# Interleaving the block sums of A21 and A22, and a different pair of first matmuls, in a Strassen-like interaction kernel

## The chip, the cores and the metric

The kernel runs on one core of a Trainium2 chip. The metric is the device time of one execution in microseconds. The engines are named as the profile names them: PE (TensorE matmul) and PEld (its weight loads), DVE (VectorE), ACT (ScalarE), POOL (GpSimd) and SP (SyncE, which here only issues DMAs).

## The reference

```python
# x: (1024, 512); weight: (64, 512, 512); lin_w: (512, 512); lin_b: (512,); all float32
out_lin = x @ lin_w.T + lin_b
xv = jnp.einsum('bf,efm->bem', x, weight)
zp = jnp.einsum('bf,efm->bem', jnp.square(x), jnp.square(weight))
interaction = 0.5 * jnp.sum(jnp.square(xv) - zp, axis=1)
return out_lin + interaction
```

Per embedding e the kernel needs the product x @ weight[e], squared and summed over the 64 embeddings. The second term is one product, x squared by the sum over e of the squared weights.

## The kernel before

All matrices are float32. The products are done with two nested levels of a Strassen (Winograd) scheme: seven block products instead of eight at each level. The x matrix is cut into four outer blocks; A21 is the one at row 1, column 0 and A22 the one at row 1, column 1. Each outer block has four inner quarters. The kernel numbers the seven left-hand operands of either level "1" to "7": "1", "2" and "4" are blocks as they are, and "5", "6", "7" and "3" are sums:

- "5" = third-row block plus fourth-row block (of a block's quarters: the raw quarter 3 plus quarter "4")
- "6" = "5" minus "1"
- "7" = "1" minus the raw quarter 3
- "3" = "2" minus "6"

So "6" needs "5", and "3" needs "6"; "7" needs only data from memory. The results lie in one resident tile `xs`, by outer and inner number. `inner_x(i)` makes the four inner sums of outer block i (lines L157 to L160, in the order 5, 6, 7, 3). Outer block "4" is A22, so `inner_x("4")` makes the sums of A22. `outer_x(i)` makes the sums of whole blocks (L144 for "5", L146 for "6", L148 for "7", L150 for "3"). All run on DVE except those of block "3", which run on POOL. A21 is not one of the seven outer operands, but the linear part needs its inner sums as well: `a21_sums` makes them on DVE (L227 to L230, tile A_sums).

The weights are handled in 32 pairs q of two embeddings. The right-hand operands come from POOL: `outer_t` makes an outer sum (tile `to`, L324) and `inner_t` the inner sums of one block (tile `ti`, three instructions, L335, L342, L343). The same three lines, called with the transposed linear weight `lw_sb`, make its inner sums `lt_sb`. `ti` and `to` have three buffers each.

The order is written out by hand. `st.at(t, fn)` files a function under a due time, and at the end all functions run in order of due time; each engine then executes its instructions in that order, one after another, waiting on semaphores where a tile needs it. Negative times are the start-up. There the order is:

1. `spin` (-40): matmuls on constants, before any data has arrived (L180 on bf16 ones, L182 on fp32 zeros). Their results are not read.
2. `lin` (-30 and -22): the linear part of the first row of outer blocks, in four PSUM banks lin0 to lin3 (L198); `lin_out` copies them out on ACT (L208).
3. `lin_p` (-14 to -2): the linear part of the second row of outer blocks, by seven products; each has one half from A21 and one from A22 (L244, banks x_lin, v_lin, y_lin). The order is 1, 5, 6, 2, 7, 3, 4. For "5" PE first takes the A21 sum, then the A22 sum. Copies between banks and out of them run on ACT (L258, L278); `lin_join` runs on DVE (L264).
4. from 0 on: the pairs, `product` (L364), with ACT copies (L429, L403, L405) and DVE additions (L408, L424) out of the banks.

The sums have these due times: inner sums of block 1 at -29, of block 2 at -22, of A21 at -20, of A22 at -18, outer and inner sums of block 5 at -16, 6 at -5, 7 at -3. POOL's order at the start is: `lt_sb` sums of both halves (-30, -29), then ti of block 1 of pair 0 (-7.5), to5, ti of block 2, to6, ti of block 6, ti of block 5.

PSUM tiles have tags: x with two buffers, v and y with three each. A tile of a tag waits until the previous holder of its buffer has been read. SP issues the loads of x in the order of `load_x` calls (L113, L109 for A21), A22 last, its raw quarter as the very last; then weights (L303, L306). ACT issues lw_sb (L120) and half of the first weights.

Of the kernel before, what the change touches and what calls it, by code (L numbers as in the profile page):

```python
# [28 lines left out]
def kernel(  # L29
# [30 lines left out]
    nc = tc.nc  # L60
    _, _, _, Q = x.shape
    E, F, M = weight.shape
    P = 128
    NK = F // P
    HM = M // 2
    BK = 2 * HM
# [20 lines left out]
    def xsl(i, o):  # L87
        return xs[:, SLOT[i], SLOT[o], :]
# [10 lines left out]
    a21 = {i: raw_sb[:, n, :] for n, i in enumerate("124")}  # L99
    a21 |= {i: a21_sb[:, n, :] for n, i in enumerate("5673")}  # L100
    A21 = raw_sb[:, 3:7, :]
# [20 lines left out]
    def quarter(r, kk, n):  # L122

        w = slice(0, 3) if n is None else n
        for i, rk in BLOCK.items():
            if rk == (r, kk):
                return a21[i] if n == 3 else xs[:, SLOT[i], w, :]
        return A21[:, w, :]

    def outer_x(i, eng=nc.vector):  # L130
        if i in BLOCK:
            return []

        def put(n):
            w = slice(0, 3) if n is None else n

            def of(o):
                return a21[o] if n == 3 else xs[:, SLOT[o], w, :]

            def src(r, kk):  # L140
                return quarter(r, kk, n)

            if i == "5":
                eng.tensor_add(of(i), src(1, 0), src(1, 1))  # L144
            elif i == "6":
                eng.tensor_sub(of(i), of("5"), src(0, 0))  # L146
            elif i == "7":
                eng.tensor_sub(of(i), src(0, 0), src(1, 0))  # L148
            else:
                eng.tensor_sub(of(i), src(0, 1), of("6"))  # L150

        return [lambda: put(None), lambda: put(3)]

    def inner_x(i, eng=nc.vector):
        add, sub = eng.tensor_add, eng.tensor_sub
        return [
            lambda: add(xsl(i, "5"), a21[i], xsl(i, "4")),  # L157
            lambda: sub(xsl(i, "6"), xsl(i, "5"), xsl(i, "1")),  # L158
            lambda: sub(xsl(i, "7"), xsl(i, "1"), a21[i]),  # L159
            lambda: sub(xsl(i, "3"), xsl(i, "2"), xsl(i, "6")),  # L160
        ]
# [10 lines left out]
    def spin():  # L172

        one = nc.const_aps.tensor(1.0, [P, BK], mybir.dt.bfloat16)
        zero = nc.const_aps.tensor(0.0, [P, BK], F32)
        for n in range(3):
            ps = psum.tile([P, BK], F32, tag="y", name=f"y_spin{n}", bufs=3)
            nc.tensor.matmul(ps, one[:, 0:P], one, start=True, stop=True)  # L180
        for n in (HM, BK):
            nc.tensor.matmul(  # L182
                ps[:, 0:n], zero[:, 0:P], zero[:, 0:n], start=True, stop=True
            )

    def lin(kk):

        order = [(s, j, l) for s in range(2) for j in range(2) for l in range(2)]
        if kk == 0:
            order.sort(key=lambda o: o[2])  # L190
        for s, j, l in order:
            n = 2 * s + j
            if kk == 0 and l == 0:
                tag = "xxvv"[n]
                LIN[n] = psum.tile(
                    [P, M], F32, tag=tag, name=f"lin{n}", bufs=2 if tag == "x" else 3
                )
            nc.tensor.matmul(  # L198
                LIN[n],
                quarter(0, kk, (0, 1, 3, 2)[2 * s + l])[:, ts(j, P)],  # L200
                lw_sb[:, 2 * kk + l, :],
                start=(kk == 0 and l == 0),
                stop=(kk == 1 and l == 1),
            )
# [10 lines left out]
    def lin_x(kk, o):  # L215
        if kk == 1:
            return xsl("4", o)
        return A21[:, SLOT[o]] if o in "124" else A21_SUMS[:, "5673".index(o)]

    def a21_sums():  # L220
        add, sub = nc.vector.tensor_add, nc.vector.tensor_sub

        def of(o):
            return lin_x(0, o)

        return [
            lambda: add(of("5"), A21[:, 3], of("4")),  # L227
            lambda: sub(of("6"), of("5"), of("1")),
            lambda: sub(of("7"), of("1"), A21[:, 3]),
            lambda: sub(of("3"), of("2"), of("6")),  # L230
        ]

    def lin_p(o, bank, first):
# [28 lines left out]
    def lin_join(bank, s, blk):  # L262
# [5 lines left out]
        return fn  # L268

    st.at(-40, spin)  # L270
    for kk in range(2):
        st.at(-30 + 8 * kk, lambda kk=kk: lin(kk))
        st.at(-30 + kk, lambda kk=kk: sums_t(LT[kk], lw_sb[:, ts(kk, 2)]))
# [256 lines left out]
    for sums, t in (  # L530
        (inner_x("1"), -29),
        (inner_x("2"), -22),
        (a21_sums(), -20),
        (inner_x("4"), -18),
        *((outer_x(m) + inner_x(m), t) for m, t in zip("567", (-16, -5, -3))),
    ):
        for n, fn in enumerate(sums):
            st.at(t + 0.1 * n, fn)
# [197 lines left out]
```

## Time and profile before

| what | value |
|---|---|
| median of 3 runs | 1421.06 us (1420.85 to 1421.62) |
| the profiled execution, its own time | 1421.11 us |
| its span, first to last instruction | 1419.3 us |
| PE busy, share of the span | 1410.8 us, 99% |
| DVE, ACT, POOL busy | 923.2, 616.9, 1179.0 us |
| mean DMA rate | 194 GB/s |

An fp32 matmul instruction of the program appears in the trace as two passes, so a product of two halves appears as a group of four. A group's line gives its start, its length, and in brackets the engine's idle time before it with what ended that; matmul ends are modelled and overlap the next start, so the distance between starts is the better measure.[...]

### The profile page before, as it was taken

How to read it: one execution, taken by the hardware profiler on the slowest of the kernel's cores; microseconds unless marked ns; L12 is line 12 of the kernel's file. 1: busy time of each engine (PE TensorE's matmuls, PEld its weight loads, DVE VectorE, ACT ScalarE, POOL GpSimd, SP SyncE). 2: the span in 40 equal slices, each digit the busy share in tenths (PEclk: the TensorE clock that was granted, in tenths of full speed). 3: DMA queues.
4: the chain of work that ended last, by engine and by line, in shares of the span. 5: the costliest groups of instructions: out<-in, count | busy, mean ns of one | idle time of the engine just before them, and what ended most of it. 6: DMA issues, size and time to landing. Idle time of an engine off the chain costs nothing.

```text
span 1419.3 us, 18121 instructions
## 1 busy us (share of the span) xinstructions
PE 1410.8 (99%) x6479; PEld 1232.5 (87%) x6479; DVE 923.2 (65%) x1338; ACT 616.9 (43%) x822; POOL 1179.0 (83%) x1046
## 2 busy tenths in 40 slices
PE   8999999999999999999999999999999999999998
PEld 5888888888888888888888888888888888888887
DVE  6766666666666665666665666665666765666665
ACT  1354443444444444444445444445444345444353
POOL 5688888888888888888888988888888888888884
PEclk9999999999999999999999999999999999999999
DMA  4399888889988889888889888899988899998884
GB/s 178 90 207 207 201 199 200 187 193 215 200 201 200 186 190 217 200 200 201 185 195 214 199 201 200 187 198 210 202 200 199 197 190 199 208 204 197 203 175 119
DMA packets 41145, 275.11 MB, mean 194 GB/s; under 512 B 4448, under 2 KB 7008, under 8 KB 8544
## 3 DMA queue, kind: packets, MB, share of 16 engines
q0 software_dynamic: 27360, 199.24, 69.0%
q1 hardware_dynamic: 12976, 72.62, 17.2%
q10 hardware_dynamic: 720, 2.10, 0.4%
q8 instruction: 52, 0.85, 0.2%
q14 instruction: 37, 0.30, 0.1%
HBM read 72.61 MB, written 2.10 MB: 53 GB/s over the span
## 4 chain that ended last, share of the span: by engine, by line
PE 98%; DVE 1%; DMA 1%; issue 0%; SPq 0%; DVEq 0%
PE y L364 41%; PE x L364 27%; PE v L364 27%; PE y_last L603 1%; DMA xs<-x 1%; PE x_last L603 0%; PE y_lin L244 0%; PE v_last L603 0%; DVE xs L160 0%; DVE xs L157 0%; PE v_lin L244 0%; DVE A_sums L230 0%; DVE xs L158 0%; PE x_lin L244 0%; DVE xs L159 0%; DVE A_sums L227 0%
## 5 line engine op out<-in xcount | busy, mean ns | idle before, releaser
L364 PE MATMUL y<-ti,xs 128*128 128x256 f32 x2688 | 653.5, 379 | 0.0
L364 PEld LDWEIGHTS y<-ti,xs 128*128 128x128 f32 x2688 | 510.6, 190 | 69.7 <-issue 0.3
L429 ACT COPY y<-x 128x512 f32<-128x512 f32 x224 | 127.7, 570 | 619.0 <-PE x L364 613.6
L364 PE MATMUL x<-to,xs 128*128 128x256 f32 x1024 | 252.3, 379 | 0.0
L364 PE MATMUL v<-ti,xs 128*128 128x256 f32 x896 | 229.9, 379 | 0.0
L364 PEld LDWEIGHTS x<-to,xs 128*128 128x128 f32 x1024 | 194.6, 190 | 26.5
L335 POOL TENSOR_TENSOR ti<-to 128x512 f32<-128x512 f32 x128 | 181.5, 1418 | 42.9 <-PE y L364 40.0
L324 POOL TENSOR_TENSOR to<-w,to 128x1024 f32<-128x1024 f32 x64 | 158.5, 2477 | 44.2 <-PE v L364 44.2
L453 ACT ACTIVATE z_c<-z_c 128x1024 f32<-128x1024 f32 x192 | 192.6, 1053 | 0.0
L364 PE MATMUL x<-w,xs 128*128 128x256 f32 x768 | 191.9, 379 | 0.0
L364 PEld LDWEIGHTS v<-ti,xs 128*128 128x128 f32 x896 | 170.2, 190 | 23.1
L424 DVE TENSOR_TENSOR z_z<-y,s 128x512 f32<-128x512 f32 x128 | 87.9, 687 | 127.5 <-PE y L364 127.5
L364 PEld LDWEIGHTS x<-w,xs 128*128 128x128 f32 x768 | 145.9, 190 | 19.8
L335 POOL TENSOR_TENSOR ti<-w 128x512 f32<-128x512 f32 x96 | 131.5, 1370 | 19.5 <-PE y L364 19.4
L364 PE MATMUL v<-to,xs 128*128 128x256 f32 x512 | 131.4, 379 | 0.0
L408 DVE TENSOR_TENSOR s<-y,z_z 128x512 f32<-128x512 f32 x160 | 110.2, 689 | 28.4 <-PE y L364 22.8
L466 POOL DMA_DIRECT2D acc<-z_c x95 | 82.8, 872 | 55.1 <-ACT z_c L453 45.7
L478 ACT ACTIVATE w<-w 128x1024 f32<-128x1024 f32 x126 | 126.3, 1053 | 0.0
L424 DVE TENSOR_TENSOR z_c<-y,s 128x512 f32<-128x512 f32 x96 | 66.4, 691 | 89.2 <-PE y L364 89.2
L408 DVE TENSOR_TENSOR s<-v,z_z 128x512 f32<-128x512 f32 x160 | 110.1, 688 | 18.0 <-PE v L364 11.0
L424 DVE TENSOR_TENSOR z_z<-v,s 128x512 f32<-128x512 f32 x128 | 87.6, 685 | 38.6 <-PE v L364 38.6
L364 PEld LDWEIGHTS v<-to,xs 128*128 128x128 f32 x512 | 97.3, 190 | 13.2
(117 smaller groups left out, 1627.1 us busy)
## 6 DMA issues: line engine op xcount, KB each, us to landing
acc<-z_c POOLq DMA_DIRECT2D x95, 1024.0 KB, 7.6
w_sum<-w POOLq DMA_DIRECT2D x63, 1024.0 KB, 8.1
w<-weight SPq DMA_DIRECT2D x62, 1024.0 KB, 6.1
acc<-z_z POOLq DMA_DIRECT2D x32, 1024.0 KB, 7.9
xq<-x SPq DMA_DIRECT2D x2, 1024.0 KB, 5.7
out<-o_last SPq DMA_DIRECT2D x8, 256.0 KB, 2.3
w<-weight ACTq DMA_DIRECT2D x2, 512.0 KB, 8.5
w<-weight SPq DMA_DIRECT2D x2, 512.0 KB, 7.7
```

The costliest lines, as they stand in the source:

```text
L324: nc.gpsimd.tensor_sub(t, a, b)
L335: nc.gpsimd.tensor_sub(t[:, 0:2, :], b[:, :, HM:M], b.rearrange("p l m -> p (l m)")[:, 0:M].rearrange("p (u c) -> p u c", u=2),)
L364: nc.tensor.matmul(ps[:, ts(j, HM)], xsl(i, o)[:, ts(j, P)], rhs, start=(start and j == 0), stop=True, skip_group_check=True,)
L408: nc.vector.tensor_add(o, d[bank], Z[q, addend][:, blk])
L424: nc.vector.tensor_add(Z[q, name][:, blk], d[bank], d[s])
L429: st.at(t0 + 0.5, lambda: nc.scalar.copy(d["y"], d["x"]))
L453: nc.scalar.activation(o, o, AF.Square)
L466: lambda: nc.gpsimd.dma_start(acc[r], Z[q, name], accum_op=ALU.add),
L478: nc.scalar.activation(w2[:, ts(h, 2)], W[q, v][:, ts(h, 2)], AF.Square)
L603: nc.tensor.matmul(ps[:, ts(j, HM)], last_x(i)[:, (0, 1, 3, 2)[2 * s + l], ts(j, P)], last_w(i)[:, l, :], start=(start and j == 0 and l == 0),
```

## The change

Three edits, all in the start-up:

- `a21_sums` and `inner_x("4")` become one list, in which the sums of A21 and A22 alternate: 5 of A21, 5 of A22, 6 of A21, 6 of A22, and so on. The last, "3" of A22, is given to POOL; the other seven stay on DVE. The list is due at -20, before the ti sums of pair 0, so in POOL's order "3" of A22 stands between the second `lt_sb` sums and ti of block 1.
- `spin` issues two 512-wide fp32 matmuls on zeros in place of three 512-wide bf16 matmuls on ones and two fp32 matmuls (256 and 512 wide) on zeros.
- the fourth `lin` bank, lin3, takes a buffer of tag y instead of v.

```diff
-        one = nc.const_aps.tensor(1.0, [P, BK], mybir.dt.bfloat16)
         zero = nc.const_aps.tensor(0.0, [P, BK], F32)
-        for n in range(3):
+        for n in range(2):
             ps = psum.tile([P, BK], F32, tag="y", name=f"y_spin{n}", bufs=3)
-            nc.tensor.matmul(ps, one[:, 0:P], one, start=True, stop=True)
-        for n in (HM, BK):
-            nc.tensor.matmul(
-                ps[:, 0:n], zero[:, 0:P], zero[:, 0:n], start=True, stop=True
-            )
+            nc.tensor.matmul(ps, zero[:, 0:P], zero, start=True, stop=True)
...
-                tag = "xxvv"[n]
+                tag = "xxvy"[n]
...
-    def a21_sums():
-        add, sub = nc.vector.tensor_add, nc.vector.tensor_sub
-
-        def of(o):
-            return lin_x(0, o)
+    def a21_a22_sums():
+        def put(kk, o, eng):
+            def of(o):
+                return lin_x(kk, o)
+
+            raw = a21["4"] if kk else A21[:, 3]
+            fn, a, b = {
+                "5": lambda: (eng.tensor_add, raw, of("4")),
+                "6": lambda: (eng.tensor_sub, of("5"), of("1")),
+                "7": lambda: (eng.tensor_sub, of("1"), raw),
+                "3": lambda: (eng.tensor_sub, of("2"), of("6")),
+            }[o]()
+            fn(of(o), a, b)
 
         return [
-            lambda: add(of("5"), A21[:, 3], of("4")),
-            lambda: sub(of("6"), of("5"), of("1")),
-            lambda: sub(of("7"), of("1"), A21[:, 3]),
-            lambda: sub(of("3"), of("2"), of("6")),
+            lambda o=o, kk=kk: put(kk, o, nc.gpsimd if o == "3" and kk else nc.vector)
+            for o in "5673"
+            for kk in range(2)
         ]
...
         (inner_x("2"), -22),
-        (a21_sums(), -20),
-        (inner_x("4"), -18),
+        (a21_a22_sums(), -20),
```

## The prediction

> **What bounds the kernel now.** I read the page's busy table first, then TensorE's waits, then busy time by stage, and last the timelines of the first 45 us, where every edit lies. TensorE (PE) is busy for 99% of the span, and its waits hold one entry inside the kernel:
>
> ```profile
> PE 1410.8 (99%) x6479; PEld 1232.5 (87%) x6479; DVE 923.2 (65%) x1338; ACT 616.9 (43%) x822; POOL 1179.0 (83%) x1046
> PE v_lin L244 <- DVE xs L157: 3.2, 1, 3.2
> ```
>
> By stage (window: length, then busy us of PE, PEld, DVE, ACT, POOL, then granted clock, DMA share, GB/s):
>
> ```profile
> 22.23:25.41 3.18, 0.00 (x0) 0.03 (x1) 3.15 (x3) 0.00 (x0) 3.02 (x3) 1.00 0.00 0
> 25.41:30.40 4.99, 4.99 (x15) 4.12 (x16) 4.66 (x9) 1.20 (x2) 1.23 (x2) 0.66 0.00 0
> 50.00:1380.00 1330.00, 1330.00 (x6164) 1170.80 (x6163) 867.00 (x1260) 593.06 (x788) 1137.02 (x1012) 1.00 0.90 198
> ```
>
> The middle of the kernel has no PE gap, so only the start can give time: PE stands still for 3.18 us and then runs 5 us at a mean clock of 0.66. The PE timeline (start, length, group of four passes) shows the same place:
>
> ```profile
> 21.20 1.03 PE L244 MATMUL v_lin<-lt_sb,A_sums 128*128 128x256 f32 x4
> 25.41 1.10 PE L244 MATMUL v_lin<-lt_sb,xs 128*128 128x256 f32 x4 [3.19 <-DVE xs L157]
> 26.35 1.45 PE L244 MATMUL y_lin<-lt_sb,A_sums 128*128 128x256 f32 x4
> 27.59 1.91 PE L244 MATMUL y_lin<-lt_sb,xs 128*128 128x256 f32 x4
> 30.63 1.03 PE L244 MATMUL x_lin<-lw_sb,xs 128*128 128x256 f32 x4
> ```
>
> At full clock groups of four start 0.863 us apart (30.63 to 36.67 is seven groups); here they are up to 1.71 apart. Why the awaited sum is late stands in the DVE and POOL timelines:
>
> ```profile
> 15.68 2.56 DVE L160 TENSOR_TENSOR xs<-xs 128x256 f32<-128x256 f32 x1
> 21.31 2.56 DVE L230 TENSOR_TENSOR A_sums<-raw_sb,A_sums 128x256 f32<-128x256 f32 x1
> 23.79 1.48 DVE L157 TENSOR_TENSOR xs<-raw_sb,xs 128x256 f32<-128x256 f32 x1
> 29.72 0.42 DVE L160 TENSOR_TENSOR xs<-xs 128x256 f32<-128x256 f32 x1
> ...
> 11.55 0.79 POOL L343 TENSOR_TENSOR lt_sb<-lw_sb,lt_sb 128x256 f32<-128x256 f32 x1
> 12.44 1.31 POOL L335 TENSOR_TENSOR ti<-w 128x512 f32<-128x512 f32 x1
> 15.44 2.52 POOL L324 TENSOR_TENSOR to<-w,w 128x1024 f32<-128x1024 f32 x1
> 21.07 2.52 POOL L324 TENSOR_TENSOR to<-w,to 128x1024 f32<-128x1024 f32 x1
> 45.68 1.27 POOL L335 TENSOR_TENSOR ti<-to 128x512 f32<-128x512 f32 x1 [18.96 <-PE y L364]
> ```
>
> The same DVE instruction takes 0.42 us when POOL is idle and 2.56 beside a 2.52 us POOL operation: from 9.5 to 26.9 one DVE sum gets through per POOL operation. The awaited A22 sum is the 13th in DVE's queue.
>
> [...]
>
> **The change, part by part.**
>
> *Eight sums reordered.* Today DVE does the four A21 sums (L227 to L230), then the four A22 sums (L157 to L160 for block 4). They now alternate, so "5" of A22 goes from 13th to 10th in DVE's queue, and "6" of A22 to 12th. With POOL busy as today these slots end at 20.5 and 23.9; PE wants the sums at 22.06 and 22.93 (below), so the order alone would leave about 1 us of wait.
>
> *"3" of A22 goes to POOL, ahead of ti_1.* It needs "6" of A22, so it is an added wait: behind it queue ti_1, to5, ti_2, to6 and ti_6.[...] POOL's lt sums end at 12.34 as today; DVE's first block ends at 12.62. From there sums start 0.34 apart, 0.46 where one reads the one just before: block 2 ends at about 14.1. Then the transfers count:
>
> ```profile
> raw_sb<-x SPq DMA_DIRECT2D x1, 512.0 KB, 10.2
> raw_sb<-x SPq DMA_DIRECT2D x1, 128.0 KB, 6.5
> ```
>
> These are A21, issued at 3.89, landing at 14.1, and the last quarter of A22, issued at 8.97, landing at 15.5 (last column: us to landing). So "5" of A21 runs at 14.2, "5" of A22 waits for the landing and runs at about 15.6, "6" of both end at about 16.7. PE wants "5" of A22 at 21.20 + 0.863 = 22.06 and "6" at 22.93: **over 6 us early**. The whole stall goes, and with it its clock loss:
> - waiting: 25.41 - 22.06 = 3.35 us;
> - half clock: 25.41 to 30.63 holds four groups, 4 x 0.863 = 3.45 of 5.22, so 1.77 us;
> - sum **5.12 us**; cross-check: 19.47 to 36.67 is 14 groups, 17.20 - 14 x 0.863 = 5.12.
>
> *POOL's delay.* The moved sum starts at about 16.75 and takes 0.8; ti_1 starts at about 17.6 instead of 12.44, 5.2 later. With today's lengths (ti three operations 3.0 to 3.1, to 2.5 to 2.6) and half a us for a 768-wide DVE sum, ti_1 ends at about 21, ti_2 at 27, to6 at 29.5, ti_6 at 32.5. PE, 5.12 earlier, wants ti_1 at 32.4, ti_2 at 36.9, to6 at 41.2 and ti_6 at 42.9. Cost nothing: the cover is POOL's 18.96 us of idleness before 45.68, of which some 8 are left. Without it each us of lateness would be a us of PE.
>
> *DVE's later queue.* Left after POOL starts are "7" of A22, "3" of A21 and six sums for block 5, one per POOL operation as today: the last rides with the last operation of ti_2, ends near 27, and the join at L264 has its bank at 33.50 - 5.12 = 28.4. PE's next write to that bank (34.95 today) is due at 29.85, the join takes 0.69: covered, with 0.75 us behind the join and 1.4 before it. The sums for blocks 6 and 7 lose about 1 us to POOL; they end near 37, when L424 (42.25 today) gets its data at 37.1. Nothing.
>
> *First matmuls.* Today:
>
> ```profile
> 0.78 1.44 PE L180 MATMUL y_spin<-const-bfloat16-1.0 128*128 128x512 bf16 x3 [0.78 <-PEq L725]
> 2.01 2.76 PE L182 MATMUL y_spin<-const-float32-0.0 128*128 128x256 f32 x4
> 4.57 2.77 PE L198 MATMUL lin<-lw_sb,xs 128*128 128x512 f32 x4
> ```
>
> A 512-wide fp32 matmul is two passes of 0.853 us at the first clock (that is the spacing from 4.57). Old: three bf16 of 0.41, two passes of 0.43, two of 0.853: 3.8 us, ending at 4.57. New: four passes, 3.41 us, ending between 4.2 and 4.5, since the first fp32 weight load (0.33) stands before it. The first lin matmul cannot come sooner: its weights wait until 4.34 for lw_sb. A gap of 0.1 to 0.4 us opens, worth nothing unless it delays the clock; a gain is excluded because PE waits again for x at 9.06. I take zero; bounds 0 and +1.4 (below).
>
> *lin3 in a y bank rather than v.* The three y buffers hold the two spins and lin3; after y_lin and y of block 1 it is y of block 2 that takes lin3's buffer; it is first written at 41.32 - 5.12 = 36.2, and lin3 is copied out by 20.3. Nothing. SP's loads of pair 1 wait for buffers that PE frees, and move with it.
>
> Sum: span 1419.3 - 5.1 = **1414.2**. This profiled execution took 1421.11, 1.8 outside the span, and the median is 1421.06, so 1416.0.
>
> **Rivals.**
> 1. *The join is late (0.20).* If DVE loses one turn, its last block-5 sum falls beside to6 (2.5 us) and ends near 29.6, the join at 30.3: PE waits about 0.5. For: eight sums meet eight POOL operations, with none to spare. Against: 1.4 us of margin. 1416.5.
> 2. *[...] (0.10).*[...] 1.4 lost: 1417.4.[...]
> 3. *Slower: the A22 transfer holds DVE and POOL (0.05).* "5" of A22 now stands ahead of all that follows on DVE, POOL waits behind it. Should its last quarter land late, PE stalls at the same matmul, clock loss included, a us per us. It decides when the landing passes 24.9 (today's sum ends at 25.3, less 0.42): at 27 the time is about 1423. Against: 15.5 in this trace, and DMA is idle from 20 on.
> 4. *No change (0.05).* A different wait before 30 costs 3 us or more and again halves the clock: 1421. I see no candidate in the profile; the instruction order of the changed kernel has the sums where the text says.
>
> **How the numbers follow.** Main case 0.60 at 1416.0. The measurement can tell about 0.2%, 2.8 us, from no change, so faster means under 1418.2: the main case and rivals 1 and 2, 0.90; same 0.05; slower 0.05. The range takes in the main case less half a us of spread and rivals 1 and 2: 1415.4 to 1417.9.
>
> **What would show it.** Right: no PE wait on L244 or its successor, clock 1.00 from 7 us on, first L364 group (36.67 today) near 31.55, DVE sums of 0.42 between 12.6 and 16.7, POOL's moved sum near 16.8, ti_1 5 us later. Wrong: a PE gap before 30, a join after 29.2, half-speed passes after 6.8, or a first L364 group later than 34.

## The result, and the profile after

The changed kernel takes 1416.09 us (median of 7 runs, 1415.46 to 1418.45), the kernel before 1420.85 beside it (7 runs, 1420.06 to 1421.93): ratio 0.9968, 95% interval 0.9957 to 0.998. The profiled execution took 1415.46 us with a span of 1413.7.

PE's busy row on the page, and then the only entry left among PE's waits:

```profile
PE 1408.3 (100%) x6476; PEld 1230.8 (87%) x6476; DVE 921.2 (65%) x1337; ACT 616.6 (44%) x822; POOL 1179.6 (83%) x1047
```

```profile
PE y_spin L179 <- PEq L728: 0.8, 1, 0.8
```

The wait of v_lin on DVE is gone. The same two windows as before (length, busy us of PE, PEld, DVE, ACT, POOL, clock, DMA share, GB/s):

```profile
22.23:25.41 3.18, 3.18 (x16) 2.80 (x15) 3.15 (x3) 1.19 (x2) 3.10 (x3) 1.00 0.00 0
25.41:30.40 4.99, 4.99 (x25) 4.38 (x24) 3.94 (x5) 0.60 (x1) 4.83 (x4) 1.00 0.01 3
```

PE is busy for all of both, at clock 1.00 where it had 0.66. Its timeline (start, length):

```profile
0.78 3.75 PE L179 MATMUL y_spin<-const-float32-0.0 128*128 128x512 f32 x4 [0.78 <-PEq L728]
4.61 2.43 PE L193 MATMUL lin<-lw_sb,xs 128*128 128x512 f32 x4
...
8.59 7.08 PE L193 MATMUL lin<-lw_sb,xs 128*128 128x512 f32 x16
...
21.53 1.03 PE L248 MATMUL v_lin<-lt_sb,xs 128*128 128x256 f32 x4
22.40 1.03 PE L248 MATMUL y_lin<-lt_sb,A_sums 128*128 128x256 f32 x4
...
31.03 1.03 PE L368 MATMUL x<-w,xs 128*128 128x256 f32 x4
```

From the start of the second row's linear part (18.94) to the first product (31.03), each group starts 0.86 us after the one before it. The first product starts at 31.03, before at 36.67: 5.64 us, and the span fell by 5.6, so the stages after the start neither gave nor took anything. PE runs lin in stages: eight passes first, then sixteen that need a further transfer of x into `xs` (here at 8.59). These sixteen are called lin's second stage below. DVE's timeline shows why, and POOL's after it:

```profile
13.26 0.42 DVE L160 TENSOR_TENSOR xs<-xs 128x256 f32<-128x256 f32 x1
13.66 0.42 DVE L229 TENSOR_TENSOR A_sums<-raw_sb 128x256 f32<-128x256 f32 x1
15.20 0.42 DVE L229 TENSOR_TENSOR xs<-raw_sb,xs 128x256 f32<-128x256 f32 x1 [1.11 <-DMA raw_sb<-x]
15.87 0.42 DVE L229 TENSOR_TENSOR xs<-xs 128x256 f32<-128x256 f32 x1
17.41 1.49 DVE L229 TENSOR_TENSOR A_sums<-raw_sb,A_sums 128x256 f32<-128x256 f32 x1
36.96 0.68 DVE L428 TENSOR_TENSOR z_z<-y,s 128x512 f32<-128x512 f32 x1
```

```profile
16.37 0.84 POOL L229 TENSOR_TENSOR xs<-xs 128x256 f32<-128x256 f32 x1 [4.10 <-DVE xs L229]
17.17 1.45 POOL L339 TENSOR_TENSOR ti<-w 128x512 f32<-128x512 f32 x1
40.04 1.27 POOL L339 TENSOR_TENSOR ti<-to 128x512 f32<-128x512 f32 x1 [7.33 <-PE y L368]
```

POOL waits 4.10 us, until 16.37, for "6" of A22. While it waits, DVE's sums take 0.42 us each; they slow down (1.49) once POOL works again. "5" of A22 is done at 15.6, where it had been done at 25.3, and what it waits for now is its transfer. POOL's idle time before ti of block 5 has shrunk from 18.96 to 7.33, because POOL came later and PE asks sooner.

### The profile page after: what moved, and what is told of

It is laid out like the page before. It is cut to its first block, busy times and chain, and to the rows that moved or that the text cites. A ratio compares the mean times of both kernels' runs of the same rounds, so it can differ in the third digit from the quotient of the medians.

```text
span 1413.7 us, 18117 instructions
## 1 busy us (share of the span) xinstructions
PE 1408.3 (100%) x6476; PEld 1230.8 (87%) x6476; DVE 921.2 (65%) x1337; ACT 616.6 (44%) x822; POOL 1179.6 (83%) x1047
## 4 chain that ended last, share of the span: by engine, by line
PE 99%; DMA 0%; DVE 0%; DVEq 0%; issue 0%
PE y L368 41%; PE v L368 27%; PE x L368 27%; PE lin L193 1%; PE y_last L606 1%; PE x_last L606 0%; PE v_last L606 0%; PE y_lin L248 0%; DMA lw_sb<-lin_wT 0%; PE x_lin L248 0%; PE v_lin L248 0%; DVE o_last L652 0%; DVE o_last L665 0%; DVE t_last L635 0%; DVEq L735 0%
## 5 line engine op out<-in xcount | busy, mean ns | idle before, releaser
L368 PEld LDWEIGHTS x<-to,xs 128*128 128x128 f32 x1024 | 194.6, 190 | 26.5
L428 DVE TENSOR_TENSOR z_z<-y,s 128x512 f32<-128x512 f32 x128 | 87.9, 687 | 125.6 <-PE y L368 125.6
L428 DVE TENSOR_TENSOR z_c<-y,s 128x512 f32<-128x512 f32 x96 | 66.4, 691 | 89.3 <-PE y L368 89.3
L428 DVE TENSOR_TENSOR z_z<-v,s 128x512 f32<-128x512 f32 x128 | 87.6, 685 | 38.2 <-PE v L368 38.2
```

The lines of the kernel that those rows point to most:

```text
L368: nc.tensor.matmul(ps[:, ts(j, HM)], xsl(i, o)[:, ts(j, P)], rhs, start=(start and j == 0), stop=True, skip_group_check=True,)
L428: nc.vector.tensor_add(Z[q, name][:, blk], d[bank], d[s])
```

## The experiments

The theory: while POOL waits, DVE's sums take 0.42 us each where they took up to 2.56 beside its operations, DVE catches up, and the stall of PE with its clock loss is gone. Rivals: the alternating order does it; the first matmuls carry part of it. All times are medians. The kernel before had medians of 1420.8 to 1421.0 beside all of these, with single executions from 1416.4 to 1422.9 (of that below). A ratio comes with its 95% interval; it is not the quotient of the two medians, which for the first experiment would be 0.9967.

**The sums alone** (sums_alone): the spins and the bank of lin3 as before.

```diff
+        one = nc.const_aps.tensor(1.0, [P, BK], mybir.dt.bfloat16)
...
-        for n in range(2):
+        for n in range(3):
...
-            nc.tensor.matmul(ps, zero[:, 0:P], zero, start=True, stop=True)
+            nc.tensor.matmul(ps, one[:, 0:P], one, start=True, stop=True)
+        for n in (HM, BK):
+            nc.tensor.matmul(
+                ps[:, 0:n], zero[:, 0:P], zero[:, 0:n], start=True, stop=True
+            )
...
-                tag = "xxvy"[n]
+                tag = "xxvv"[n]
```

> Only the reordered sums with '3' of A22 on POOL; first matmuls and the bank of lin3 as in the kernel before. Theory ([...]the PE stall of 3.35 us and its 1.77 us of half clock go): the whole gain, about 1416.0, no PE wait on v_lin. Rival (the shorter first matmuls carry part of it, since lin started its second stage 0.5 us sooner after the change): about 1416.5 and lin's second stage at 9.1.

1416.05 us (1415.75 to 1416.32, 10 runs), ratio 0.9975 (0.9965 to 0.9984). No PE wait on v_lin. The sums carry all of it that can be measured. Lin's second stage began at 8.9 here. Over the traces it began at 8.74 to 9.41 with the old spins and at 8.55 to 10.00 with the new ones, so the 8.59 in the changed kernel cannot be put down to the new spins.

**The first matmuls and the bank alone** (spin_alone): against the kernel before, only

```diff
-        for n in range(3):
+        for n in range(2):
...
-            nc.tensor.matmul(ps, one[:, 0:P], one, start=True, stop=True)
-        for n in (HM, BK):
-            nc.tensor.matmul(
-                ps[:, 0:n], zero[:, 0:P], zero[:, 0:n], start=True, stop=True
-            )
+            nc.tensor.matmul(ps, zero[:, 0:P], zero, start=True, stop=True)
...
-                tag = "xxvv"[n]
+                tag = "xxvy"[n]
```

> Only the two fp32 first matmuls and lin3 in a y bank; sums as in the kernel before. Theory: no effect, 1420.9 within 0.5, the stall of 3.2 us on v_lin still there. Rival: 0.5 us faster, because the first passes end sooner; or 1.4 slower if the gap of a few tenths before lin delays the clock.

1419.01 us (1417.91 to 1422.65, 13 runs), ratio 0.9999 (0.999 to 1.0008): no difference that the comparison can tell, though the median is 1.75 us lower (1420.76 beside it). The stall stayed; PE's timeline of the profiled execution (1419.33 us):

```profile
25.31 1.10 PE L239 MATMUL v_lin<-lt_sb,xs 128*128 128x256 f32 x4 [3.17 <-DVE xs L157]
26.25 1.03 PE L239 MATMUL y_lin<-lt_sb,A_sums 128*128 128x256 f32 x4
27.11 1.03 PE L239 MATMUL y_lin<-lt_sb,xs 128*128 128x256 f32 x4
```

Here, after the same stall of 3.17 us, the clock was **not** halved: it was 1.00 from 25.31 to 30.40, and the later groups follow 0.86 apart. The time is 1.8 us below the profiled execution of before, about its clock loss. So that loss does not follow from the length of the stall alone.

**POOL's wait without the alternation** (hold_in_old_order): first the four A21 sums, then those of A22, the last on POOL.

```diff
-            for o in "5673"
-            for kk in range(2)
+            for kk in range(2)
+            for o in "5673"
```

> The changed kernel, but the four A21 sums first and then those of A22, the last still on POOL ahead of ti_1. Theory (the hold on POOL does it, not the order): DVE runs at 0.34 to 0.46 us a sum while POOL waits, the A21 sums end near 15.1, '5' of A22 still waits for its transfer at 15.2, so 1416.1, same as the changed kernel. Rival (the alternation does it): '5' of A22 is 13th again, PE stalls at v_lin, 1418 or more.

1415.9 us (1415.44 to 1416.33, 8 runs), as the changed kernel. The DVE timeline from the last A21 sum on:

```profile
14.89 0.42 DVE L229 TENSOR_TENSOR A_sums<-raw_sb,A_sums 128x256 f32<-128x256 f32 x1
15.23 0.42 DVE L229 TENSOR_TENSOR xs<-raw_sb,xs 128x256 f32<-128x256 f32 x1
15.68 0.42 DVE L229 TENSOR_TENSOR xs<-xs 128x256 f32<-128x256 f32 x1
```

"5" of A22, 13th again, starts at 15.23, no later than as tenth, because all four A21 sums fit into the time until its transfer has landed (15.20 in the changed kernel's trace). The alternation is worth nothing that can be measured while POOL waits.

**The alternation without POOL's wait** (all_dve): "3" of A22 on DVE.

```diff
-            lambda o=o, kk=kk: put(kk, o, nc.gpsimd if o == "3" and kk else nc.vector)
+            lambda o=o, kk=kk: put(kk, o, nc.vector)
```

> The changed kernel, but '3' of A22 on DVE, so POOL does not wait; the alternation stays. Theory: DVE again gets one turn per POOL operation; '5' of A22 ends near 20.0 in time for 21.5, '6' of A22 near 23.4 to 23.9 for 23.3, so PE waits 0.1 to 0.6 us there; the sums for block 5 end near 29.7, the join at L268 near 30.4 for a PE write at 29.3, so 1.1 us more: about 1417.6[...]. Rival (the alternation is the gain): 1416.1, no PE wait.

1417.07 us (1416.63 to 1417.47, 19 runs), 1.0 above the changed kernel. DVE's timeline, PE's wait, and PE's timeline at the two places:

```profile
21.13 2.57 DVE L229 TENSOR_TENSOR xs<-xs 128x256 f32<-128x256 f32 x1
29.89 0.68 DVE L268 SCALAR_TENSOR_TENSOR acc<-y_lin,s_lin 128x512 f32<-128x512 f32 x1
```

```profile
PE y_lin L248 <- DVE acc L268: 0.5, 1, 0.5
```

```profile
22.75 1.03 PE L248 MATMUL y_lin<-lt_sb,A_sums 128*128 128x256 f32 x4
23.85 1.10 PE L248 MATMUL y_lin<-lt_sb,xs 128*128 128x256 f32 x4
...
29.10 1.03 PE L248 MATMUL v_lin<-lw_sb,xs 128*128 128x256 f32 x4
30.63 1.13 PE L248 MATMUL y_lin<-lt_sb,raw_sb 128*128 128x256 f32 x4 [0.50 <-DVE acc L268]
```

"6" of A22 again sits out a 2.5 us POOL operation and ends at 23.7 (PE's group, due at 23.61, starts at 23.85), and the join at L268 is late. By the distances between starts, less the 0.863 of a group, these cost PE 0.24 and 0.67 us, without clock loss. So the order alone removes most of the stall, the wait alone all of it, and beside the wait the order has nothing left to do. The edit that makes POOL wait also takes one sum off DVE. That sum stands behind "5" and "6" of A22 in either order, so it cannot have made them earlier; its share in the join was not tried apart.

**Shorter first matmuls** (short_spin): two bf16 matmuls on ones, in place of the fp32 ones, in the changed kernel.

```diff
-        zero = nc.const_aps.tensor(0.0, [P, BK], F32)
+        zero = nc.const_aps.tensor(1.0, [P, BK], mybir.dt.bfloat16)
```

> The changed kernel, but the two first matmuls are bf16 on ones (two passes of 0.41 us at the first clock in place of four of 0.853), so PE idles from about 1.6 to 4.6 ahead of lin. Theory[...]: the first fp32 matmuls are worth about 1.4 us; without them lin runs at half speed up to about 9.5 instead of 6, and the time is about 1417.5. Rival (they only set up the y banks, the clock comes up anyway): 1416.1.

1416.94 us (1415.95 to 1417.78, 14 runs), against 1416.09 of the changed kernel in the same comparison (10 runs): 0.85 us. PE's timeline of the profiled execution:

```profile
4.08 3.50 PE L193 MATMUL lin<-lw_sb,xs 128*128 128x512 f32 x4 [2.28 <-DMA lw_sb<-lin_wT]
7.42 1.88 PE L193 MATMUL lin<-lw_sb,raw_sb 128*128 128x512 f32 x4
```

The direction is the theory's, the size smaller: the half-speed passes (0.85 us apart, 0.43 afterwards) end at about 7.4, not 9.5, and PE's first four lin passes take 3.3 us from start to the next group, where they took 2.3. The 9.5 and the 1.4 us were my estimate, which no trace had shown. This execution (1415.95) is the fastest of the fourteen; the slower ones were not traced, so the 0.85 us rests on the medians, and how it comes about in them is not shown.

**POOL later still** (pool_x8, pool_x16): "3" of A22 computed eight or sixteen times.

```diff
-            fn(of(o), a, b)
+            for _ in range(8 if o == "3" and kk else 1):
+                fn(of(o), a, b)
```

> The changed kernel with '3' of A22 computed eight times on POOL, so ti_1 and all that follows on POOL comes some 6 us later. Theory (7.3 us of POOL idleness before ti of block 5 cover the delay): no change, 1416.1, the idle time before ti of block 5 falls to about 1.5 us. Rival (POOL's lateness already costs): up to 6 us more.

> The same sum sixteen times, POOL some 12 to 13 us later. Theory: the cover is gone; ti_1 ends near 33.4 where PE wants it at 31.9, so PE waits about 1.5 us there and some tenths at ti_2: 1418 to 1419.5. Rival (POOL catches up in a later gap): 1416.1.

Eight times: 1419.86 us (1418.36 to 1420.67, 13 runs), so my expectation of no change was **wrong** by 3.8. Sixteen times: 1422.29 us (1421.35 to 1425.54, 16 runs), 2.8 us above the range that I had expected, and not by the wait for ti_1 (ti of block 1) that I had named. PE's waits, first of eight, then of sixteen:

```profile
PE y L369 <- DVE z_z L429: 2.4, 1, 2.4
...
```

```profile
PE y L369 <- DVE z_z L429: 3.3, 1, 3.3
PE v_lin L249 <- POOL xs L230: 2.3, 1, 2.3
...
```

PE waits for DVE, and with sixteen for the repeated sum itself, but not for ti. DVE's timeline with eight shows the path:

```profile
33.83 2.57 DVE L159 TENSOR_TENSOR xs<-xs,a_sb 128x256 f32<-128x256 f32 x1
36.33 1.49 DVE L160 TENSOR_TENSOR xs<-xs 128x256 f32<-128x256 f32 x1
41.65 0.69 DVE L429 TENSOR_TENSOR z_z<-y,s 128x512 f32<-128x512 f32 x1
```

POOL's to6 and ti_6, 7 us later, now lie beside DVE's sums for block 6; a 0.42 us sum takes 2.57, and L429 runs at 41.65 where PE wanted its bank at 39.9. The wait alone, added to the changed kernel's 1416.09, gives 1418.45; six of the thirteen executions took 1418.36 to 1418.63, at a mean clock of 1.0 over the run. The other seven took 1419.86 to 1420.67 at 0.998 or 0.999. One of these is the profiled execution (1420.67), in which half clock followed (0.53 from 42.39 to 46.00), as PE's timeline shows by a group of 2.07:

```profile
42.39 2.07 PE L369 MATMUL y<-ti,xs 128*128 128x256 f32 x4 [2.36 <-DVE z_z L429]
```

ti_1 to ti_6 themselves were in time. With sixteen, the two waits (2.3 and 3.3 us) make up most of the 6.2 us. The first of them was followed by no half clock in the profiled execution; the groups go on at 0.97 and 0.86 apart:

```profile
31.91 1.13 PE L249 MATMUL v_lin<-lw_sb,xs 128*128 128x256 f32 x4 [2.30 <-POOL xs L230]
32.88 1.03 PE L249 MATMUL y_lin<-lt_sb,raw_sb 128*128 128x256 f32 x4
33.74 1.03 PE L249 MATMUL y_lin<-lt_sb,xs 128*128 128x256 f32 x4
```

**The kernel before, twice more** (before_again, before_third).

> The kernel before, one more profiled execution, for the spread of its times (1416.4 to 1422.9). Theory: the PE stall of 3.2 us ahead of v_lin is there each time[...]: about 1419.1 or 1420.9. Rival: the stall itself comes and goes.

> The kernel before, one more profiled execution, as above: the stall of about 3.2 us each time, with or without the half clock (1420.9 or 1419.1). Rival: the stall itself comes and goes.

1422.75 and 1420.74 us. Both show the stall of 3.19 us. PE's timeline in the first:

```profile
25.73 2.04 PE L244 MATMUL v_lin<-lt_sb,xs 128*128 128x256 f32 x4 [3.19 <-DVE xs L157]
27.56 1.91 PE L244 MATMUL y_lin<-lt_sb,A_sums 128*128 128x256 f32 x4
...
32.29 1.03 PE L244 MATMUL x_lin<-lw_sb,xs 128*128 128x256 f32 x4
```

Four groups take 6.56 us, at a mean clock of 0.53, where full clock needs 3.45: 3.1 lost. In the other it is 1.77, as in the profile shown at first. With spin_alone, the same stall of 3.2 us cost 0.1, 1.8, 1.8 and 3.1 us of clock in four executions.

**The changed kernel again, and the rest of the start** (after_again, lw_late).

> The changed kernel itself beside the three others, as their measure: 1416.1, within half a us.

1416.09 us (1415.69 to 1418.58, 10 runs). Its profiled execution happened to be the slowest, and shows what the changed kernel still pays at times:

```profile
5.91 1.88 PE L193 MATMUL lin<-lw_sb,raw_sb 128*128 128x512 f32 x4
10.00 8.80 PE L193 MATMUL lin<-lw_sb,xs 128*128 128x512 f32 x16 [2.22 <-DMA xs<-x]
```

The part of x that lin's second stage needs (quarters 1 and 2 of the first outer block, x(0,0)) landed at 9.96, PE stood 2.22 us, and the sixteen passes took 8.80 us in place of 7.08 (clock 0.80). That landing lay between 8.5 and 10.0 in all traces up to then. So the last kernel moves 512 KB that lin needs only for its second half out of its way:

```diff
     load_x(0, 1, slice(0, 3), 3)
+    nc.sync.dma_start(lw_sb[:, 2:4], lw_src[:, 2:4])
     load_x(1, 0, slice(0, 4))
     load_x(1, 1, slice(0, 3), 3)
-    for k in (slice(0, 1), slice(1, 2), slice(2, 4)):
+    for k in (slice(0, 1), slice(1, 2)):
```

> The changed kernel with the second half of the linear weights (lw_sb 2:4, 512 KB) loaded on SP's queue after block (0,1) of x, not third on ACT's queue. Theory (what is left at the start is the landing of x(0,0) quarters 1 and 2, at 8.5 to 10.0 in the traces so far, because 0.5 MB not needed before 12 us shares the DMA engines with it): it lands near 7.8, the PE gap ahead of lin's second stage goes, 0.7 us saved: 1415.4, and a narrower spread. Rival (that landing is set by something else, or lin's second half then waits for lw_sb): 1416.1 or slower.

1415.23 us (1414.68 to 1415.63, 6 runs), ratio to the kernel before 0.9964 (0.9951 to 0.9978). PE's timeline:

```profile
6.16 1.88 PE L194 MATMUL lin<-lw_sb,raw_sb 128*128 128x512 f32 x4
7.88 7.03 PE L194 MATMUL lin<-lw_sb,xs 128*128 128x512 f32 x16
```

In this execution x lands at 6.9, the second stage follows the first without a gap, and the first product starts at 30.27. It is the fastest version here, 0.9 us under the changed kernel; it was not run in one comparison with it, and the intervals against the kernel before overlap.

## Why the prediction was right, and where it was not

- *The stall goes.* Right, and DVE caught up during POOL's wait, as predicted. What makes a DVE sum longer beside a POOL operation was not shown, only that it was (2.56 us against 0.42). "3" of A22 started on POOL at 16.37 (predicted 16.75), "5" of A22 at 15.20 (15.6), held by the transfer named. hold_in_old_order and all_dve separate the two halves of the edit: the prediction's "the order alone would leave about 1 us of wait" was 0.24 us at y_lin and another 0.67 at the join, 1.0 in the time.
- *5.12 us.* The medians differ by 4.8, the two profiled spans by 5.6. The 3.35 us of waiting is in all four traces with the old sums. The **1.77 us of half clock is not a constant**: I took it from one execution, and it is 0.1 to 3.1 with the same stall. That its size came near is partly the luck of that profile. Even the waiting cannot have been whole in every execution: some of the kernel before took under 1417.2 us (see what is left open).
- *First matmuls, zero.* No effect that the comparison resolves. My reason "PE waits again for x at 9.06" took a landing of one execution as fixed; it moved between 8.5 and 10.0, which is the 0.5 us by which all of the profile after ran ahead of the predicted times (first product 31.03 against 31.55).
- *lin3's bank.* Nothing, as predicted. It was not tried apart from the spins.
- *POOL's delay costs nothing.* True: ti_1 ended at 20.9 (about 21), ti_2 at 26.5 (27), ti_6 at 32.7 (32.5). But the cover named, POOL's idle 8 us, is not the one that counts. pool_x8 started ti_1 some 7 us later, still left POOL 4.68 us of idleness there, and lost 3.8 us, through DVE sums beside POOL operations that had moved, the path that the prediction's paragraph on DVE's later queue priced at 1 us. In the changed kernel L428 ran at 36.96 with no idle time of DVE before it; that was the tighter margin.
- *Rival 1 (late join)* did not occur: 27.86, with 1.05 us of idle before it. all_dve showed it near the price given, 0.5 us in the list of waits and 0.67 by the starts. *Rival 2 (at 1417.4: lin starts with more passes at half speed)* did not occur: from 6.87 on lin's passes start 0.43 us apart, in the kernel before from 7.18. Its 1.4 us was my estimate, not shown by a trace; short_spin put the worth of the early matmuls at 0.85. *Rival 3* did not occur: A22's last quarter had landed by 15.2 (16.5 in after_again), far ahead of the 24.9 named. A late transfer did hold PE, but another one, outside the change: x(0,0) ahead of lin's second stage, for 2.2 us, with a clock of 0.80 after it, in one execution. That is the 1418.58; the 1418.45 of the first comparison was not traced. *Rival 4*, a different wait of 3 us or more before 30, did not occur.

Left open: four of 40 executions of the kernel before in one comparison took 1416.4 to 1417.0, and three of 41 in another 1416.7 to 1417.2, nearly as fast as the changed kernel. No trace has caught one. The stall without clock loss comes to 1419.3, or 1418.9 with the earliest landing of x that was traced before the last kernel (8.5 in place of 8.96), so these executions must have had less of the stall.

A possible cause is the number of sums that DVE gets through before POOL starts its second group of `lt_sb` sums. In the four traces with the old sums one ran at 0.42 to 0.43 us and the second already took 1.37 beside POOL (9.06 and 9.52, POOL from 9.23). In the changed kernel's two traces two ran undisturbed (8.53 and 8.99, POOL from 9.07). One turn gained would let "5" of A22 end where the 12th sum ends in the profile before, at 23.9 instead of 25.3; two turns, at 21.4, with "6" at 23.9 for a PE that wants it at 22.93. By this estimate the times are 1419.3 - 1.4 = 1417.9 and 1419.3 - 2.4 = 1416.9. No trace shows it.

Whether the new first matmuls make the half clock rarer (6 of 13 spin_alone runs, 12 of those 40, were under 1418.8) is not settled.

## What to carry to other kernels

Before moving a small sum, look at what the other engines run at that time: here a 0.42 us sum took 2.56 beside another engine's operation, and an added wait on that engine was the gain, because it left the first undisturbed for 4 us at the moment that mattered. When an engine's queue is delayed, check not only who needs its results but whose instructions it will then run beside. A loss read from one profile, like a halved clock after a gap, should be taken as a range until a second execution shows it again.

## What the runs showed of the hardware that I had not expected

- One and the same gap of 3.2 us in PE's work was followed by 0.1 to 3.1 us of loss in four traces. Gaps of 2.22 us (after_again) and 2.36 us (pool_x8) were followed by a lower clock in the traced executions (0.80 over 8.64 us, 0.53 over 3.61 us); one of 2.30 us (pool_x16) was not (groups 0.97 and 0.86 us apart).
- The landing of one 256 KB transfer early in the kernel varied by 1.4 us between executions of the same loads (8.52 to 9.96 over twelve), and came at 6.9, in one trace, once 512 KB had been moved behind it.
